# A four-layer graph network on one core: exponentials without a bias column, attention's gathered products one chunk later, feature copies apart from their transposes

## The chip, the cores and the metric

The kernel runs on one core of one Trainium2 chip. The core has a matrix engine (TensorE, PE in the profile, with its weight loads as PEld), a vector engine (DVE), an engine for functions and copies (ScalarE, ACT), a general engine (GpSimd, POOL), and a queue engine (SyncE, SP) that here starts transfers. Each engine works through its own instructions strictly in order, and waits on the others by semaphores. Transfers started on SP's and POOL's queues run on 16 DMA engines.

The metric is the device time of one execution in microseconds. The time before the change is the median of three executions, 1510.31 us (1508.68 to 1513.79).

## The reference, cut to what matters

Input are features `x` (4096 nodes, 64 features) and a symmetric, sparse weight matrix `adj` of 4096 x 4096. Four layers follow, each wrapped as `x = layernorm(x + layer(x, adj))`:

```python
# layer 0: Chebyshev polynomial of adj
terms = [x, L @ x]
for _ in range(2, 4): terms.append(2 * (L @ terms[-1]) - terms[-2])
return einsum('kni,kio->no', stack(terms), weight)

# layer 1: two gated cells, one fed by sums over neighbours, one by attention
edge_output = gru_cell(node_support, h, w_ih_e, w_hh_e, b_ih_e, b_hh_e)
edge_support = softmax(scores by the sign of adj) * adj @ (h @ W)
node_output = gru_cell(edge_support, h, w_ih_n, w_hh_n, b_ih_n, b_hh_n)

# layer 2: each neighbour weighted by 0.5 ** (rank from the last one)
w = mask * where(pos > 0, 0.5 ** (k - pos), 0)
return w @ (x @ weight) + bias

# layer 3: hyperbolic aggregation
log_ij = logmap(x_i, x_j)            # arctanh of a norm, for every pair i, j
agg = einsum('ij,ijc->ic', adj / deg, log_ij)
return expmap(0, agg @ weight + bias)
```

In the last layer every one of the 4096 x 4096 pairs needs a factor with a square root and an inverse hyperbolic tangent. The kernel forms them from a pair's number v: w = v squared less one, its root by a logarithm and an exponential of half of it, the logarithm of v plus the root, and the inverse root by another exponential.

## The kernel before, in words

The matrix is handled in 8 groups of 512 rows by 8 chunks of 512 columns, tiles of 128 x 4 x 512 numbers (1 MB). The program is written in an order, but a scheduler places the instructions on each engine by its own estimate of when they are ready; instructions wrapped in `in_order` keep their written order among each other. An engine then never leaves the placed order. So an edit can move instructions that it doesn't touch.

*Layer 0* (to about 570 us). PE transposes every tile (L633), ACT copies it out (L640), POOL's queue stores it (L664), and three passes of products follow; in the third, the groups of rows are taken from both ends (7, 0, 6, 1, 5, 2, 4, 3). When a group's pass is over, `third_weighed` weighs its sum (ACT copies the bank out to `t_h` at L545, PE multiplies at L552, DVE adds at L708). One chunk later `after_third` calls `normed_third`: PE turns the sum back (L492), DVE and ACT make the layer norm (root on ACT, L265), DVE centres the features in `nat_a` (L315) and splits them in three parts (L236 to L244, with a scratch tile `sp_rest`, tag `t0`). Four chunks after that `turned_third` calls `turn_pairs` (L226): POOL sets a column to one (L229), ACT copies the group's features to `with_ones` (L230), PE transposes them in pairs (L233), ACT copies them out (L234). `with_ones` shares tag `t0` and its two buffers with `sp_rest`. The last group (3) does this within attention, as its fourth step.

*Attention, layer 1* (to about 850 us). Per group of rows, over 8 chunks: DVE makes the masks `pos` (L477), POOL's queue stores them (L773), PE accumulates `p_ps` (L1041, L1049) and `a_ps` (L1058). After a group, `group_end` gives six parts of work, one for each following chunk (`steps_of`, L1001; popped at L1097). Part one: gates of the edge cell for two halves h of the group (PE L835, L842; tanh on ACT L851; the rest on DVE L856 to L858), scores and their exponentials (L906, L907), `gathered` of half 0 (PE, L932), shares (DVE, to L925), new state. Part two: `shared` of half 0 (ACT copies with a scale, L941), `gathered` and `shared` of half 1, gates of the node cell (PE L835) and their sum (DVE L865). The results of gates and of `gathered` go in turn to the two buffers of the tag `post`, each of two banks, so that half 0 of `gathered` follows half 0 of the edge gates in one buffer, and half 0 of the node gates follows half 0 of `gathered`.

*Layer 2* (to about 1050 us). Here `seam` holds small steps of other work, one taken per block of columns (L1345): first the last group's `group_end`, each step by itself. While `seam` isn't empty (`busy`, L1344), both evictions of `cnt_ps` per half block are on ACT (L1320), else one of them is on DVE (L1322).

*Layer 3* (to the end). 36 tiles on and above the diagonal, two units of 128 x 1024 each (8 of the 72 units are half as large). Per unit: PE forms v (L1435), ACT squares it (L1444), PE adds a very large number to pairs on opposite sides of the unit sphere (L1454), DVE subtracts one with a floor (L1462), ACT takes the logarithm (L1633) and the exponential of its half (L1634), DVE adds v (L1658), ACT takes the inverse root by an exponential (L1660) and the logarithm (L1669), DVE clips and multiplies (L1643), multiplies into `adj` (L1646) and into its transposed copy (L1482, after transposes L1480), and PE sums (L1496, L1508). So that numbers stay in the logarithm's domain, its input is scaled by 2^-20 and each exponential gives that back by a bias read from a column in memory, `half_shift`.

Of the kernel before, what the change touches and what calls it, by code (L numbers as in the profile page):

```python
# [9 lines left out]
F32 = mybir.dt.float32  # L10
# [3 lines left out]
AF = mybir.ActivationFunctionType  # L14
ALU = mybir.AluOpType
# [6 lines left out]
MIN_NORM = 1e-15  # L22
# [5 lines left out]
V_FLOOR = 2.0**-21  # L28

OPPOSITE = 2.0**60  # L30

# [6 lines left out]
TANH_ONE = 20.0  # L38
LN_SHIFT = 20

# [20 lines left out]
def gnn4_kernel(  # L61
# [21 lines left out]
    nc = tc.nc  # L83
    P = 128
    N, F = x.shape
    NB = N // P
    GB = 4
# [44 lines left out]
    nc.vector.memset(neg_inf, NEG_INF)  # L132
    half_shift = const.tile([P, 2], F32, name="half_shift")
    nc.vector.memset(half_shift[:, 0:1], 0.5 * LN_SHIFT * math.log(2.0))
    nc.vector.memset(half_shift[:, 1:2], -0.5 * LN_SHIFT * math.log(2.0))
    one_col = const.tile([P, 1], F32, name="one_col")
    nc.vector.memset(one_col, 1.0)

    pair = const.tile([P, F], F32, name="pair")
# [69 lines left out]
    def gblocks(g):  # L209
        return slice(g * GB, (g + 1) * GB)  # L210
# [8 lines left out]
    def to_rows(pool, src, w):  # L219
# [4 lines left out]
        return ps  # L224

    def turn_pairs(pool, g):  # L226

        t = sm.tile([P, GB, F], F32, name="with_ones", tag="t0")
        nc.gpsimd.memset(t[:, :, F - 1], 1.0)  # L229
        nc.scalar.copy(t[:, :, 0 : F - 1], nat_a[:, gblocks(g), 0 : F - 1])  # L230
        ps = pool.tile([P, GB // 2, P], F32, name="post", tag="post")
        for m in range(GB // 2):
            nc.tensor.transpose(ps[:, m, :], t[:, 2 * m : 2 * m + 2, :].rearrange("p b f -> p (b f)"), ident)  # L233
        nc.scalar.copy(tr_x[:, g * GB // 2 : (g + 1) * GB // 2, :], ps)  # L234
# [249 lines left out]
    def mine(g):  # L484

        return slice(g % 2 * F, g % 2 * F + F)
# [18 lines left out]
    with tc.tile_pool(name="acc", bufs=1) as acc_p, tc.tile_pool(  # L505
# [204 lines left out]
        def after_third(g):  # L710
            normed_third(g, acc_t[mine(g), g // 2, :], ps_p)

        def turned_third(g):
# [93 lines left out]
    def group_end(g, Q, nb, tl, sums, a_t, wq, by_ln=False):  # L807
# [179 lines left out]
        def of(h, *parts):  # L987
            return lambda ps_p: [part(ps_p, h) for part in parts]

        return [  # L990
            [of(0, edge_gates)], [of(0, edge_tanh)], [of(0, edge_rest), of(1, edge_gates)], [of(1, edge_tanh)],
            [of(1, edge_rest), scores], [tanh_n, score_exps, of(0, gathered)], [shares],
            [lambda ps_p: new_state(edge)],
        ], [
            [of(0, shared), of(1, gathered)], [of(1, shared)], [of(0, node_gates)], [of(0, node_sum)],
        ], [
# [8 lines left out]
    def attention(signed, cols_p, sg, tl, ps_a, ps_p):  # L1005
# [67 lines left out]
        ahead = [masks(*order[n]) for n in range(lead)]  # L1073
        steps = [nothing, nothing, nothing, lambda ps_p: turn_pairs(ps_p, last_row)]
        for n, (g, c) in enumerate(order):
# [83 lines left out]
    def constants3():  # L1159
# [12 lines left out]

        nc.vector.tensor_scalar(w[:, 0 : F - 1], pair[:, 0 : F - 1], 1.0, -4.0, ALU.add, ALU.mult)
        nc.vector.tensor_scalar(w[:, 0 : F - 1], w[:, 0 : F - 1], not_last, None, ALU.mult)
        nc.vector.tensor_copy(w[:, F - 1 : F], pair[:, F - 1 : F])
        nc.vector.memset(to_right, 0.0)
# [191 lines left out]
    with tc.tile_pool(name="o3", bufs=1) as op, tc.tile_pool(name="cols3", bufs=3) as cols_p, tc.tile_pool(  # L1368
# [90 lines left out]
        def less_one(n):  # L1459
            if n < NU:  # L1460
                w = ws[n][:, :, columns(n)]
                nc.vector.tensor_scalar(w, w, -1.0, V_FLOOR * (V_FLOOR + 2.0), ALU.add, ALU.max)  # L1462

# [58 lines left out]
        def factors(ps_p):  # L1522

            t = sm.tile([P, NB], F32, name="plus")
            nc.vector.tensor_scalar_max(t, deg, 1e-8)
            nc.vector.reciprocal(t, t)
            plus = sm.tile([P, NB], F32, name="plus")
            nc.vector.tensor_scalar_max(plus, inside, MIN_NORM)
            nc.vector.tensor_tensor(t, t, plus, ALU.mult)
            nc.vector.tensor_copy(kappa[:, 1, :], t)  # L1530
            nc.vector.tensor_tensor(t, t, rabs, ALU.mult)
            nc.vector.tensor_tensor(kappa[:, 0, :], t, inside, ALU.mult)
# [88 lines left out]
        while n < NU + 2 or turns or gathers:  # L1621
# [5 lines left out]
            if n < NU:  # L1627
                if n % 2 == 0:
                    fs[n // 2] = fp.tile([P, CB, GW], F32, name="f3")
                w, cs = ws[n][:, :, columns(n)], columns(n)  # L1630
                rts[n] = el.tile([P, HB, GW], F32, name="rt3")
                rt = rts[n][:, :, cs]
                nc.scalar.activation(w, w, AF.Ln, scale=2.0**-LN_SHIFT)  # L1633
                nc.scalar.activation(rt, w, AF.Exp, bias=half_shift[:, 0:1], scale=0.5)  # L1634
                square(n + 1)
                opposite(n + 1)
# [20 lines left out]
            if n < NU:  # L1657
                nc.vector.scalar_tensor_tensor(rt, vs[n][:, :, cs], 1.0 + V_FLOOR, rt, ALU.max, ALU.add)  # L1658
                product(n + 2)
                nc.scalar.activation(w, w, AF.Exp, bias=half_shift[:, 1:2], scale=-0.5)  # L1660
            late = turn(late_turns.pop(n)) if n in late_turns else []
# [5 lines left out]
            if 0 < n <= NU:  # L1667
                rt = rts[n - 1][:, :, columns(n - 1)]
                nc.scalar.activation(rt, rt, AF.Ln)  # L1669
            if seam:  # L1670
# [56 lines left out]
```

## Time and profile before

| | |
|---|---|
| median of three executions | 1510.31 us |
| the profiled execution | 1508.28 us |
| its span, first to last instruction | 1506.2 us |
| PE busy | 1366.3 us, 91% |
| DVE busy | 1030.4 us, 68% |
| ACT busy | 764.6 us, 51% |
| POOL busy | 123.2 us, 8% |
| chain that ended last | PE 55%, ACT 16%, DVE 16%, DMA 7% |

The profile comes from one execution. Its page gives each engine's busy time, its busy tenths in 40 slices of the span, the chain of work that ended last (followed back from the last instruction to what released it), and the costliest groups of instructions. A group's row reads: line, engine, operation, output from input, shapes, count, busy time, mean of one in ns, and the idle time just before it with what ended it. Other views give the busy time of each engine within a window, who waited for whom, and the timeline. The shares of the whole span are means over stages with different limits: ACT's 51% is under 30% in attention and over 90% in the last layer.

### The profile page before, as it was taken

To read this page: it belongs to the slowest core of one execution; us is meant where nothing else is said; L and a number is where in the kernel's file an instruction comes from. 1 tells how busy PE (TensorE), PEld (TensorE's weight loads), DVE (VectorE), ACT (ScalarE), POOL (GpSimd) and SP (SyncE) were. 2 spreads that over 40 slices of the span, in tenths; PEclk is the share of its full clock that TensorE was granted. 3 is DMA by queue.
4 is the path that set the end of the run, shared out by engine and by line. 5 is a ranking of instruction groups with operands and counts; after the bars stand their busy time and mean duration, and the time that the engine had idled before them with its cause. 6 is when DMAs were issued, how large, how long until landed. Compare 5 with 4: busy or idle time off the path is not lost.

```text
span 1506.2 us, 19544 instructions
## 1 busy us (share of the span) xinstructions
PE 1366.3 (91%) x7124; PEld 609.0 (40%) x7124; DVE 1030.4 (68%) x2008; ACT 764.6 (51%) x1301; POOL 123.2 (8%) x206
## 2 busy tenths in 40 slices
PE   5899999999999989888999999999788889888894
PEld 3555555564444323333333332333233334344342
DVE  5999999885000556666776422444999999999995
ACT  3554444442000111122222277564789999999993
POOL 4101000000000002222222100000000000000000
PEclk8999999999999999999999999999899999999997
DMA  9999999996678898888988655551434453544420
GB/s 292 415 406 413 411 411 400 387 353 273 238 280 272 344 403 308 290 299 296 338 328 312 207 171 174 169 168 58 196 140 171 160 204 140 202 165 171 154 105 11
DMA packets 103361, 385.40 MB, mean 256 GB/s; under 512 B 16340, under 2 KB 17368, under 8 KB 71256
## 3 DMA queue, kind: packets, MB, share of 16 engines
q1 hardware_dynamic: 84256, 296.78, 55.0%
q0 software_dynamic: 15616, 85.73, 13.9%
q10 hardware_dynamic: 3384, 1.56, 0.4%
q8 instruction: 58, 0.95, 0.3%
q14 instruction: 47, 0.39, 0.1%
HBM read 297.26 MB, written 85.20 MB: 254 GB/s over the span
## 4 chain that ended last, share of the span: by engine, by line
PE 55%; ACT 16%; DVE 16%; DMA 7%; issue 3%; SPq 1%; ACTq 0%; POOL 0%; DVEq 0%; POOLq 0%
PE tp L633 7%; PE pass L541 7%; PE w_ps L541 6%; PE a_ps L1058 4%; PE pass L534 4%; PE cnt_ps L1315 4%; DMA raw<-in_adj_dram 4%; PE acc_ps L1271 3%; PE h_ps L534 3%; PE p_ps L1041 2%; ACT w L1633 2%; PE post L552 2%; ACT rt L1634 2%; ACT rt L1669 2%; DVE at_m L1482 2%
## 5 line engine op out<-in xcount | busy, mean ns | idle before, releaser
L640 ACT COPY at<-tp 128x512 f32<-128x512 f32 x256 | 132.5, 600 | 132.3 <-issue 93.2
L1320 ACT ACTIVATE wt<-cnt_ps 128x512 uint16<-128x512 f32 x206 | 114.6, 596 | 72.2 <-PE cnt_ps L1315 67.9
L1496 PE MATMUL sums_ps<-at_d,nat_c 128*64 128x512 f32 x288 | 145.6, 628 | 3.0 <-DVE at_d L1475 2.0
L633 PE MATMUL tp<-ident,raw 128*128 128x128 f32 x1024 | 131.9, 282 | 15.2 <-DMA raw<-in_adj_dram 10.1
L666 DVE TENSOR_REDUCE dpart<-raw 128x4 f32<-128x2048 f32 x64 | 145.5, 2273 | 0.1
L668 DVE TENSOR_REDUCE lows<-raw 128x1 f32<-128x2048 f32 x64 | 145.4, 2272 | 0.0
L633 PEld LDWEIGHTS tp<-ident,raw 128*128 128x128 f32 x1024 | 115.0, 143 | 54.8 <-issue 30.2
L1058 PE MATMUL a_ps<-at,nat_a 128*64 128x512 f32 x512 | 126.3, 621 | 2.9 <-DVE at L1024 2.9
L477 DVE TENSOR_SCALAR pos<-at 128x2048 fp8e4<-128x2048 f32 x72 | 87.7, 1234 | 50.0 <-DMA at<-adj_t 43.8
L1508 PE MATMUL sums_ps<-at_m,nat_c 128*64 128x512 f32 x224 | 111.5, 621 | 0.0
L1435 PE MATMUL v_ps<-rv,tr_a 64*128 64x512 f32 (+1 forms) x288 | 82.8, 654 | 28.0 <-DVE rt L1658 27.5
L541 PE MATMUL w_ps<-at,cheb_n 128*128 128x512 f32 x224 | 101.1, 595 | 0.0
L541 PE MATMUL pass<-at,cheb_n 128*128 128x512 f32 x224 | 100.0, 604 | 0.7 <-DVE cheb_n L694 0.7
L1658 DVE SCALAR_TENSOR_TENSOR rt<-v_ps,rt 128x1024 f32<-128x1024 f32 x72 | 83.6, 1163 | 9.0 <-ACT rt L1634 8.8
L1315 PE MATMUL cnt_ps<-m,follow 128*64 128x512 fp8e4 x480 | 81.5, 391 | 4.8 <-ACT wt L1320 1.7
L1643 DVE SCALAR_TENSOR_TENSOR f<-rt,w 128x1024 f32<-128x1024 f32 x72 | 83.1, 1163 | 3.9 <-ACT rt L1669 3.9
L1646 DVE TENSOR_TENSOR at_d<-at_d,f 128x1024 f32<-128x1024 f32 x72 | 83.6, 1161 | 0.2
L1322 DVE TENSOR_SCALAR wt<-cnt_ps 128x512 uint16<-128x512 f32 x50 | 34.6, 692 | 67.9 <-PE cnt_ps L1315 67.9
L1634 ACT ACTIVATE rt<-w,half_shift 128x1024 f32<-128x1024 f32 x72 | 78.9, 1100 | 0.5
L1660 ACT ACTIVATE w<-w,half_shift 128x1024 f32<-128x1024 f32 x72 | 78.8, 1098 | 0.5
L1482 DVE TENSOR_TENSOR at_m<-post,at_m 128x512 f32<-128x512 f32 x112 | 74.4, 685 | 4.5 <-PE post L1480 4.5
L1480 PE MATMUL post<-ident,f 128*128 128x128 f32 x448 | 68.1, 284 | 9.5 <-DVE at_m L1482 8.5
(396 smaller groups left out, 2228.8 us busy)
## 6 DMA issues: line engine op xcount, KB each, us to landing
at<-adj_t SPq DMA_DIRECT2D x122, 1024.0 KB, 5.9
raw<-in_adj_dram SPq DMA_DIRECT2D x64, 1024.0 KB, 13.1
adj_t<-at POOLq DMA_DIRECT2D x64, 1024.0 KB, 8.1
at_d<-adj_t SPq DMA_DIRECT2D x36, 1024.0 KB, 4.8
at_m<-adj_t SPq DMA_DIRECT2D x28, 1024.0 KB, 7.0
mask_t<-pos POOLq DMA_DIRECT2D x64, 256.0 KB, 5.7
m<-mask_t SPq DMA_DIRECT2D x120, 128.0 KB, 2.8
m<-mask_t SPq DMA_DIRECT2D x60, 256.0 KB, 4.1
```

What stands on the lines that cost most here:

```text
L534: in_order(nc.tensor.matmul(ps[q * F : (q + 1) * F, :], lhsT=cheb_n[:, jb, k, :], rhs=rhs, start=first, stop=last, skip_group_check=True,))
L541: in_order(nc.tensor.matmul(ps, lhsT=cheb_n[:, jb, k : k + 2, :], rhs=rhs, start=first, stop=last))
L633: in_order(nc.tensor.transpose(tp[:, cols(b)], raw[:, b, cols(k)], ident))
L640: nc.scalar.copy(at[:, k, :], tp)
L666: in_order(nc.vector.tensor_reduce(dpart[:, g, c, :], raw, AX.X, ALU.add))
L668: in_order(nc.vector.tensor_reduce(lows[:, n : n + 1], raw.rearrange("p b j -> p (b j)"), AX.X, ALU.min))
L1058: in_order(nc.tensor.matmul(ps[q * F : (q + 1) * F, :], lhsT=nat_a[:, c * CB + k, 0:F], rhs=parts[q if signed else 0][:, k, :], start=(c = ...
L1315: in_order(nc.tensor.matmul(cnt[a][r * HP : (r + 1) * HP, :], lhsT=follow, rhs=chunks[c][odd][2 * a + r][:, k, :], start=(h == 2 * NB - 1) ...
L1320: in_order(nc.scalar.activation(wt[odd][a], cnt[a], AF.Relu, scale=-128.0))
L1496: in_order(nc.tensor.matmul(bank[0:F, :], lhsT=nat_c[:, j * CB + k, :], rhs=own[t][:, k, :], start=(i == j and k == 0), stop=(j == seq[-1] ...
L1508: in_order(nc.tensor.matmul(bank[F:P, :], lhsT=nat_c[:, above * GB + k, :], rhs=mirrored[tm][:, k, :], start=(k == 0 and above == seq[0]), ...
L1634: nc.scalar.activation(rt, w, AF.Exp, bias=half_shift[:, 0:1], scale=0.5)
```

## The change

In the last layer v itself is scaled by 2^-10 (in the small weights that PE uses for it, `constants3`), so that its square carries 2^-20 and no shift is needed: logarithm and exponentials lose scale and bias, the column `half_shift` goes, and the constants that v and w meet carry the scale, as does the last logarithm (an immediate scale). The number for opposite pairs is 2^50, not 2^60.

In `group_end`, `gathered` of half 0 moves from part one to the front of part two, a chunk later; in layer 2's seam it is a step of its own, and the shift by one step moves two evictions of `cnt_ps` from DVE to ACT.

`turn_pairs` is cut in two: `put_ones` (the fill and the copy to `with_ones`) is called right after `normed_third`, and the transposes stay where they were written. `with_ones` gets a tag and two buffers of its own.

```diff
-OPPOSITE = 2.0**60
+OPPOSITE = 2.0**50
-LN_SHIFT = 20
+SCALE = 2.0**-10
...
-    half_shift = const.tile([P, 2], F32, name="half_shift")
-    nc.vector.memset(half_shift[:, 0:1], 0.5 * LN_SHIFT * math.log(2.0))
-    nc.vector.memset(half_shift[:, 1:2], -0.5 * LN_SHIFT * math.log(2.0))
...
-    def turn_pairs(pool, g):
-        t = sm.tile([P, GB, F], F32, name="with_ones", tag="t0")
+    ones_in = {}
+    def put_ones(g):
+        ones_in[g] = t = sm.tile([P, GB, F], F32, name="with_ones")
         nc.gpsimd.memset(t[:, :, F - 1], 1.0)
         nc.scalar.copy(t[:, :, 0 : F - 1], nat_a[:, gblocks(g), 0 : F - 1])
+    def turn_pairs(pool, g):
+        t = ones_in[g]
...
         def after_third(g):
             normed_third(g, acc_t[mine(g), g // 2, :], ps_p)
+            put_ones(g)
...
-            [of(1, edge_rest), scores], [tanh_n, score_exps, of(0, gathered)], [shares],
-            [lambda ps_p: new_state(edge)],
+            [of(1, edge_rest), scores], [tanh_n, score_exps], [shares], [lambda ps_p: new_state(edge)],
         ], [
-            [of(0, shared), of(1, gathered)], [of(1, shared)], [of(0, node_gates)], [of(0, node_sum)],
+            [of(0, gathered)], [of(0, shared), of(1, gathered)], [of(1, shared)], [of(0, node_gates)], [of(0, node_sum)],
...
-        steps = [nothing, nothing, nothing, lambda ps_p: turn_pairs(ps_p, last_row)]
+        steps = [nothing, nothing, lambda ps_p: put_ones(last_row), lambda ps_p: turn_pairs(ps_p, last_row)]
...
-        nc.vector.tensor_scalar(w[:, 0 : F - 1], pair[:, 0 : F - 1], 1.0, -4.0, ALU.add, ALU.mult)
+        nc.vector.tensor_scalar(w[:, 0 : F - 1], pair[:, 0 : F - 1], 1.0, -4.0 * SCALE, ALU.add, ALU.mult)
...
-                nc.vector.tensor_scalar(w, w, -1.0, V_FLOOR * (V_FLOOR + 2.0), ALU.add, ALU.max)
+                nc.vector.tensor_scalar(w, w, -SCALE * SCALE, V_FLOOR * (V_FLOOR + 2.0) * SCALE**2, ALU.add, ALU.max)
...
-            nc.vector.tensor_scalar_max(plus, inside, MIN_NORM)
+            nc.vector.tensor_scalar(plus, inside, MIN_NORM, SCALE, ALU.max, ALU.mult)
...
-                nc.scalar.activation(w, w, AF.Ln, scale=2.0**-LN_SHIFT)
-                nc.scalar.activation(rt, w, AF.Exp, bias=half_shift[:, 0:1], scale=0.5)
+                nc.scalar.activation(w, w, AF.Ln)
+                nc.scalar.activation(rt, w, AF.Exp, scale=0.5)
...
-                nc.vector.scalar_tensor_tensor(rt, vs[n][:, :, cs], 1.0 + V_FLOOR, rt, ALU.max, ALU.add)
+                nc.vector.scalar_tensor_tensor(rt, vs[n][:, :, cs], (1.0 + V_FLOOR) * SCALE, rt, ALU.max, ALU.add)
...
-                nc.scalar.activation(w, w, AF.Exp, bias=half_shift[:, 1:2], scale=-0.5)
+                nc.scalar.activation(w, w, AF.Exp, scale=-0.5)
...
-                nc.scalar.activation(rt, rt, AF.Ln)
+                nc.scalar.activation(rt, rt, AF.Ln, scale=1.0 / SCALE)
```

More of the change, by code (lines that the diff above doesn't have):

```diff
@@ L1171, in constants3 @@
         nc.vector.tensor_scalar(not_last, pair[:, F - 1 : F], -1.0, 1.0, ALU.mult, ALU.add)
-        nc.vector.tensor_scalar(w[:, 0 : F - 1], pair[:, 0 : F - 1], 1.0, -4.0, ALU.add, ALU.mult)
+        nc.vector.tensor_scalar(w[:, 0 : F - 1], pair[:, 0 : F - 1], 1.0, -4.0 * SCALE, ALU.add, ALU.mult)
         nc.vector.tensor_scalar(w[:, 0 : F - 1], w[:, 0 : F - 1], not_last, None, ALU.mult)
-        nc.vector.tensor_copy(w[:, F - 1 : F], pair[:, F - 1 : F])
+        nc.vector.tensor_scalar_mul(w[:, F - 1 : F], pair[:, F - 1 : F], SCALE)
         nc.vector.memset(to_right, 0.0)
```

## The prediction

> **What bounds the kernel now.** I read the page first (span, engines, slices), then windows around each place that the change touches, then who waited for whom there, then single stretches of the timeline.
>
> ```profile
> span 1506.2 us, 19544 instructions
> ...
> PE   5899999999999989888999999999788889888894
> DVE  5999999885000556666776422444999999999995
> ACT  3554444442000111122222277564789999999993
> ```
>
> TensorE (PE) is at eight tenths or more in 37 of 40 slices; from slice 29 on (about 1060 us, the last layer) DVE and ScalarE (ACT) are at nine tenths too, and PE has its waits. The busy times of that stretch, 1060 to 1470 us (columns: length, then busy us of PE, PEld, DVE, ACT, POOL, then clock and DMA), and who DVE waited for there:
>
> ```profile
> 1060.00:1470.00 410.00, 356.51 (x1695) 151.58 (x1691) 385.51 (x651) 391.40 (x533) 0.62 (x2) 0.96 0.43 162
> ```
> ```profile
> DVE rt L1658 <- ACT rt L1634: 8.8, 10, 2.8
> DVE w L1462 <- ACT w L1444: 5.6, 8, 1.4
> DVE f L1643 <- ACT rt L1669: 3.9, 6, 1.1
> DVE at_m L1482 <- PE post L1480: 3.7, 6, 1.3
> ```
>
> ACT is idle 18.6 of 410 us, DVE 24.5: two engines almost equally full, and DVE's waits are mostly for ACT (18.3 of them). The chain that ended last in this stretch, by line (the answer breaks off there):
>
> ```profile
> by line: ACT w L1633 8.5%; ACT rt L1634 8.3%; ACT rt L1669 8.1%; DVE at_m L1482 7.5%; ACT w L1660 7.3%; DVE rt L1658 7.0%; PE sums_ps L1496 6.8%; ACT w L1444 6.7%; DVE at_d L1646 5.6%; DVE f L1643 5.1%; issue 5.0%; PE v_ps L1435 4.1%; DVE w
> ```
>
> The exponentials L1634 and L1660 hold 15.6% of it. In attention (580 to 845 us) PE is the bound but for stretches at 570 to 685 us that end on loads; its waits there, and one group's timeline (start, length, instruction):
>
> ```profile
> ACT gin L941 <- DVE share L925: 16.2, 7, 2.4
> ...
> PE post L932 <- DVE n L858: 11.5, 7, 3.0
> ```
> ```profile
> 754.14 0.89 PE L932 MATMUL post<-wq,a_t 128*128 128x192 f32 x4 [1.12 <-DVE n L858]
> ...
> 758.13 0.81 PE L932 MATMUL post<-wq,a_t 128*128 128x192 f32 x4
> 758.93 0.70 PE L835 MATMUL post<-whh_n,tr_a 64*128 64x256 f32 x4
> ```
> ```profile
> 755.25 0.30 ACT L907 ACTIVATE none<-top,neg_inf 128x4 f32<-128x4 f32 x1 [0.20 <-DVE top L900]
> 755.65 0.21 ACT L906 ACTIVATE share<-share 128x4 f32<-128x4 f32 x1
> 758.14 1.58 ACT L941 ACTIVATE gin<-post,share 128x192 f32<-128x192 f32 x4 [2.29 <-DVE share L925]
> ```
>
> The reader is to see that node gates (L835) stand ready to start just when ACT has emptied the first gathered bank. In the third pass (500 to 570 us) PE waits little, 4.2 us of it for the features' copy:
>
> ```profile
> 551.35 0.41 PE L233 MATMUL post<-ident,with_ones 128*128 128x128 f32 x2 [3.17 <-ACT with_ones L230]
> ```
> ```profile
> 550.80 0.40 ACT L230 COPY with_ones<-nat_a 128x252 f32<-128x252 f32 x1 [4.38 <-DVE sp_lo L244]
> ```
>
> **The change part by part.**
>
> *Exponentials without bias.* L1634 and L1660, 72 each, lose the per-partition bias. Price: in the timeline above two exponentials of 128x4 stand side by side, 0.30 us with a bias column, 0.21 without. At 128x1024, where ACT runs without a gap, one instruction starts 1.04 us after an exponential with bias and 0.948 us after a logarithm without, so 0.093 us each. 144 of them: 13.4 us of ACT's time. The other edits here (constants in L1462, L1658, L1669, the scale in `factors` and `constants3`) leave count, shapes and engines as they are; two small fills at the start go, off any path. What of 13.4 us reaches the end? First way: the chain has 15.6% of 410 us = 64 us in these lines, 61 instructions of 1.04, so 61 x 0.093 = 5.7. Second way: ACT's busy time falls to 378.0, below DVE's 385.5; if the fuller engine stays idle as long as now (18.6), the stretch takes 404.1, 5.9 less. What is late next is DVE, with PE's waits for L1658 behind it. I take 6. Ends: 13.4 (ACT alone bounds) and below nothing, because the order of instructions in this layer is remade on ACT, DVE and PE: the logarithm L1669 follows its own L1634 and L1660 at once in 5 places, not 1, where DVE's 1.22 us between them doesn't fit under 0.95; ACT's waits of this kind are 6.0 us in 7 now, 0.86 each, so 4 more are +3.4. Against that, L1633 stands one instruction behind its square L1444 in 7 places, not 14. I put the order at nothing.
>
> The Trainium skill, "Perfetto Trace Analysis", section "Identifying the Most-Contended Engine", has the engine of highest occupancy as the one whose relief pays; read strictly, ACT with 95.5% against DVE's 94.0% would return all 13.4 us, and the sum below would be -13.9. The waits shown above, with DVE only 5.9 us less busy, speak against so much.
>
> *Gathered products one chunk later.* `gathered` of half 0 (two products, four passes, no DMA) leaves the step behind edge gates and stands with half 1 in the next chunk. Orders of DVE, ACT, POOL and SP in the branch that runs stay as they are. PE's wait of 1.12 us goes (11.5 in 7 groups). But node gates of half 0 write the bank that gathered half 0 has just filled, and it is emptied by ACT's first two L941, which wait for the shares, and these for DVE's L925, ending at 758.03. Nothing of that moves: the second L941 ends at 758.88. PE would reach L835 at 758.93 - 1.12 = 757.8 and wait until about 758.95. The same holds at 645, 720, 788 and 821 us: nothing won in five groups. In the two others, where the wait is 2.87 and 3.04 (at 606 and 685), L835 stands at 612.58 and 691.33, while L941's second copy ends at 610.88 and 689.66: 1.6 won in each, 3.2; loads are awaited soon after (at 629 and 664 PE waits 2.0 and 2.9 for DVE behind them), so I count half, -1.5. Ends: -11.5 and +0.7 (0.1 of signalling in each of seven).
>
> *Copies apart from transposes.* `put_ones` (a fill of 0.11 on POOL, a copy of 0.40 on ACT) comes four chunks ahead, in buffers of its own, so it no longer waits for `sp_lo` (L244). On POOL two fills go ahead of layer 0's stores, which wait for ACT anyway (214 us); in attention the fill stays behind the third mask store, and its buffer's last reader is two rows back. Not free: the order of PE changes, the transposes L233 stand one chunk earlier, and ACT's queue has the copy ahead of the root L265 and of `t_h` (L545). Rows 6 and 1: the turn of row 1 (L492) now stands directly behind L552, and waits for DVE's L708, which ends at 522.3: 0.8. Row 6's transposes are reached at about 524.7, while its features are centred at 525.1 and copied by 525.7: 1.1; row 1's about 0.45. Old waits 0.76 and 0.27 go: +1.3. Rows 5 and 2: the copy of row 5 can start at 541.3 (L315 ends 541.2) and is ahead of the `t_h` copy that ran at 540.35: PE is 1.35 late. The 3.17 wait shrinks to about 1.1, as row 2 is centred 5 us after its L492, with one transposing step and one chunk of 3.65 between: -2.1, so -0.7. Sum +0.6, taken as +1, since DVE's interleaving of two rows changes as well. Ends: -4.2 (all waits go, none comes) and +4.8 (0.8 + 1.1 + 0.45 + 1.35 + 1.1, none goes).
>
> *Layer 2's seam* runs 26 small steps, not 25. Two evictions of 0.69 go from DVE to ACT (0.60 each). ACT is busy 85 of 140 us in 900 to 1040, PE 136: nothing, and up to 1.2 if PE waited for both.
>
> Sum: -6 - 1.5 + 1 = -6.5. The profiled execution took 1508.28 us (2.1 beside its span), so 1501.8; it lies 2.0 under the median of 1510.31, so 1503.8 for the median.
>
> **The rivals.**
> 1. *ACT bounds the last layer alone.* For: ACT's idle time of 18.6 us is the smallest. Against: DVE at 385.5. It gives -13.4 - 1.5 + 1 = -13.9: 1496.4. Chance 0.20.
> 2. *DVE takes over at once,* and ACT's gain turns into waits of ACT for L1658 and L1462. For: DVE's 94%. Against: DVE waits 18.3 us for ACT. With 1 us won there: -1.5, 1508.8. Chance 0.19.
> 3. *Attention's waits do go,* as the change's words suggest: -11.5 in place of -1.5, 1493.8. It needs shares ahead of 757; nothing in DVE's order brings that. Chance 0.06.
> 4. *Slower: the remade order of the last layer.* In-order queues block where ACT's instruction stands ahead of what DVE can feed it. It decides when a unit (there are 72) loses over 0.15 us, as 72 x 0.15 = 10.8 outweighs 6 and leaves +4.5 or so: 1514.8 and above, say 1516. Against it is the shorter list of tight places. Chance 0.08.
>
> **How the numbers follow.** About 0.3%, 4.5 us, is what a measurement of this kernel can tell from no change. The forecast has 0.47; its own range, from the 4 to 8 us that the last layer may return and 2 either way elsewhere, is 1499 to 1508, and a seventh of it lies within 0.3% (above 1505.8). Faster: 0.40 + 0.20 + 0.06 = 0.66. Same: 0.07 + 0.19 = 0.26. Slower: 0.08. The range reaches to 1493 (rival 1 with 3 us more from the third pass) and to 1510 (rival 2 and a little): it leaves out most of rival 4 and the far ends.
>
> **What would show it.** After: exponentials of 128x1024 at 1.05 us like the logarithms; ACT busy near 378 and DVE near 385 in a last layer of about 404 us; no wait of PE on L932, and in its place one of about 1.1 us on node gates for ACT's `gin`; a period of 33.7 us per group as now (754.14 to 787.84); the third pass as long as now or 1 us longer. Wrong if the last layer shortens by over 10 us or under 2, or if the groups' period falls by 1 us.

## The result and the profile after

| | before | after |
|---|---|---|
| median, timed together | 1509.06 us (6 executions) | 1497.12 us (6 executions, 1492.16 to 1503.91) |
| ratio, 95% interval | | 0.9931 (0.9907 to 0.9955) |
| once more, in a later set of runs: medians | 1507.59 us (35) | 1501.34 us (12, 1492.48 to 1507.66) |
| ratio, 95% interval | | 0.9944 (0.9920 to 0.9968) |
| profiled execution, its span | 1508.28, 1506.2 us | 1492.16, 1490.4 us |

The change makes the kernel faster by 8 to 10 us, where 6.5 were forecast. The two profiled executions differ by 16 us. That is more than the change gives: the profiled execution of after is the fastest of 18, and other executions of the same program ran up to 15 us longer. So stages are compared below over all profiled executions that share the part in question, not between two.

The page of the changed kernel: span, and the busy tenths of three engines in 40 slices.

```profile
span 1490.4 us, 19538 instructions
...
PE   5999999999999989889999899999788899889884
...
DVE  5989998886000467666677422435899999999995
ACT  3554444342000110222222277564789999999993
```

The picture is the old one: PE nearly full to slice 28, then DVE and ACT at nine tenths. The last layer (first product L1439 to last logarithm L1673) in this execution: length, then busy us of PE, PEld, DVE, ACT, POOL, clock, DMA share, GB/s.

```profile
1051.40:1454.40 403.00, 353.53 (x1706) 151.49 (x1705) 385.93 (x657) 380.39 (x530) 0.62 (x2) 0.98 0.44 168
```

The costliest groups of ACT there, and then who DVE waited for there (us in total, times, longest):

```profile
L1664 ACT ACTIVATE w<-w 128x1024 f32<-128x1024 f32 x72 | 72.3, 1006 | 0.7
L1638 ACT ACTIVATE rt<-w 128x1024 f32<-128x1024 f32 x72 | 72.3, 1005 | 0.6
```
```profile
DVE w L1466 <- ACT w L1448: 5.4, 6, 1.8
DVE rt L1662 <- ACT rt L1638: 3.4, 5, 2.5
DVE at_m L1486 <- PE post L1484: 3.2, 3, 1.4
DVE f L1647 <- ACT rt L1673: 2.1, 4, 0.6
```

An exponential takes as long as a logarithm now; the two groups lost 13.1 us (78.9 + 78.8 before). DVE, whose work is unchanged (387.3 before, over 412.1 us), is now the fuller engine, and its waits for ACT's first exponential fell from 8.8 to 3.4.

In attention, the timeline of one group shows the wait in its new place. PE's products (L937, now both halves together) no longer wait; its node gates (L840) do, for ACT's `gin`:

```profile
749.91 1.46 PE L937 MATMUL post<-wq,a_t 128*128 128x192 f32 x8
752.71 0.70 PE L840 MATMUL post<-whh_n,tr_a 64*128 64x256 f32 x4 [1.34 <-ACT gin L946]
```
```profile
751.92 1.36 ACT L946 ACTIVATE gin<-post,share 128x192 f32<-128x192 f32 x4 [2.29 <-DVE share L930]
```

The stages, in us. "Attention, loads" runs from the first group's copy of `p_t` to the fourth's, "steady" from there to the eighth's. Means; the number of profiled executions and their range in brackets. An execution is counted for a stage where that stage has the part in question and no other edit.

| stage | without the part | with it | difference | forecast |
|---|---|---|---|---|
| second and third pass, first `t_v` copy to the first `p_ps` | 193.9 (3: 193.7 to 194.2) | 192.8 (11: 192.6 to 194.2) | -1.1 | +1 |
| attention, loads | 114.7 (3: 113.4 to 116.0) | 111.7 (8: 109.4 to 114.1) | -3.0 | -1.5 |
| attention, steady | 134.9 (3) | 134.9 (8: 134.7 to 135.6) | 0 | 0 |
| layer 2 | 208.5 (3: 205.9 to 210.6) | 209.4 (8: 205.9 to 210.6) | +0.9, in the spread | 0 |
| last layer | 412.2 (4: 411.5 to 412.8) | 405.4 (6: 403.0 to 406.8) | -6.8 | -6 |
| from there to the end | 37.5 (4: 36.7 to 38.5) | 35.9 (6: 35.6 to 36.0) | -1.7 | 0 |

These differences sum to -11.7; the times say -10.4 (-14.0 to -6.8) and -8.4 (-12.1 to -4.8).

Part of this is the granted clock. In these traces it is 1.00 or 0.50 and nothing between, and it falls for 3.4 us at a time or for several times that; 3.4 us at half clock are 1.7 us of PE's work lost. In "attention, loads", where PE has waits of up to 3.9 us, the time at half clock orders all fourteen profiled executions:

| at half clock | length of "attention, loads" |
|---|---|
| 3.4 us | 109.4 |
| 6.8 us | 110.7 to 112.7 (6 executions) |
| 10.2 us | 113.3, 113.4 |
| 11.8 us | 114.1 |
| 13.7 us | 114.6, 116.0 (the latter the kernel before) |
| 20.5 us | 120.6, 120.8 (two experiments below, "both halves in one buffer") |

Layer 2 is 205.9 us long where the clock never falls, 208.9 to 209.3 with 6.8 us at half clock and 210.3 to 210.6 with 10.2.

### The profile page after: what moved, and what is told of

Read it like the earlier page. It is cut to its first block, busy times and chain, and to the rows that moved or that the text cites. A ratio compares the mean times of both kernels' runs of the same rounds, so it can differ in the third digit from the quotient of the medians.

```text
span 1490.4 us, 19538 instructions
## 1 busy us (share of the span) xinstructions
PE 1355.1 (91%) x7124; PEld 609.0 (41%) x7124; DVE 1026.1 (69%) x2004; ACT 753.2 (51%) x1303; POOL 122.7 (8%) x206
## 4 chain that ended last, share of the span: by engine, by line
PE 51%; DVE 20%; ACT 16%; issue 6%; DMA 5%; ACTq 1%; POOL 0%; SPq 0%; DVEq 0%; POOLq 0%
PE tp L637 7%; PE pass L545 7%; PE w_ps L545 7%; PE cnt_ps L1319 4%; PE acc_ps L1275 4%; PE pass L538 3%; PE h_ps L538 3%; PE post L556 2%; DVE at_m L1486 2%; ACT w L1637 2%; DMA at<-adj_t 2%; DVE f L1647 2%; ACT w L1448 2%; ACT rt L1638 2%; ACT wt L1324 2%
## 5 line engine op out<-in xcount | busy, mean ns | idle before, releaser
L1500 PE MATMUL sums_ps<-at_d,nat_c 128*64 128x512 f32 x288 | 140.6, 607 | 2.4 <-DVE at_d L1479 1.8
L1062 PE MATMUL a_ps<-at,nat_a 128*64 128x512 f32 x512 | 122.4, 605 | 2.9 <-DVE at L1028 2.9
L1512 PE MATMUL sums_ps<-at_m,nat_c 128*64 128x512 f32 x224 | 107.3, 600 | 0.0
L1439 PE MATMUL v_ps<-rv,tr_a 64*128 64x512 f32 (+1 forms) x288 | 79.4, 629 | 22.6 <-DVE rt L1662 22.4
L1673 ACT ACTIVATE rt<-rt 128x1024 f32<-128x1024 f32 x72 | 72.4, 1005 | 9.5 <-DVE rt L1662 9.2
L1637 ACT ACTIVATE w<-w 128x1024 f32<-128x1024 f32 x72 | 72.0, 1002 | 5.0 <-DVE w L1466 5.0
```

Of the source, the lines that this page charges most:

```text
L1062: in_order(nc.tensor.matmul(ps[q * F : (q + 1) * F, :], lhsT=nat_a[:, c * CB + k, 0:F], rhs=parts[q if signed else 0][:, k, :], start=(c = ...
L1500: in_order(nc.tensor.matmul(bank[0:F, :], lhsT=nat_c[:, j * CB + k, :], rhs=own[t][:, k, :], start=(i == j and k == 0), stop=(j == seq[-1] ...
L1512: in_order(nc.tensor.matmul(bank[F:P, :], lhsT=nat_c[:, above * GB + k, :], rhs=mirrored[tm][:, k, :], start=(k == 0 and above == seq[0]), ...
```

## The experiments

Each ratio is to the kernel before, run on the same chip in the same set, with its 95% interval. Line numbers of an experiment can be one to three off those of the changed kernel; the operations tell which is which.

### Each part alone

**The exponentials and scales alone**: the kernel before with all hunks of the diff that concern `SCALE`, `OPPOSITE` and `half_shift`.

> The kernel before with the edits of the exponentials and scales alone; attention and the third pass as before. From the two traces: 9 us under the kernel before, all of it in the last layer. By the prediction's term: 6 under. If only the whole change gains that much there: less than 4 under.

Measured: median 1499.89 us, ratio 0.9938 (0.9921 to 0.9955), that is -9.4 us (-11.9 to -6.8). Last layer 403.5, end of it to end of program 36.0. This part alone gives as much as the whole change.

**The gathered products alone**:

```diff
-            [of(1, edge_rest), scores], [tanh_n, score_exps, of(0, gathered)], [shares],
-            [lambda ps_p: new_state(edge)],
+            [of(1, edge_rest), scores], [tanh_n, score_exps], [shares], [lambda ps_p: new_state(edge)],
...
-            [of(0, shared), of(1, gathered)], [of(1, shared)], [of(0, node_gates)], [of(0, node_sum)],
+            [of(0, gathered)], [of(0, shared), of(1, gathered)], [of(1, shared)], [of(0, node_gates)], [of(0, node_sum)],
```

> The kernel before with the gathered products one chunk later alone; last layer in the old order with the old price. By the prediction: 1.5 us under the kernel before, half a us to 1.6 in each of the two groups whose loads bind (stretches of 606 and 685 us). From the two traces: about 5 under, 2 and 3 in those two groups, nothing in the other groups, where PE's wait of 1.1 moves from the gathered products to the node gates and becomes 1.3. Nothing in the other stages.

Measured: 1507.38 us, ratio 1.0005 (0.9980 to 1.0030). Loads stretch 112.7, 1.9 under the mean of those without it; steady groups 135.6. In the time the part is nothing that can be told, and 5 us are excluded. What the two profiles seemed to show here (-5.2 over attention) was mostly the spread of the groups that wait for loads: with the same order of instructions they took anything from 109.4 to 114.1 us.

In the two load-bound groups where the forecast had 1.6 us each to win, PE's waits of 2.87 and 3.04 came back in full at the node gates, 2.87 and 3.25. What the part won in the first of them is mostly the clock's. In the kernel before, the products behind the wait took 3.46 us; without the wait in front of them the same eight took 1.94 (the kernel before, then this one):

```profile
606.14 0.89 PE L932 MATMUL post<-wq,a_t 128*128 128x192 f32 x4 [2.87 <-DVE n L858]
606.96 3.46 PE L1058 MATMUL a_ps<-at,nat_a 128*64 128x512 f32 x8
```
```profile
602.94 1.94 PE L1057 MATMUL a_ps<-at,nat_a 128*64 128x512 f32 x8
```

**The copies apart from their transposes alone** (`put_ones` and its calls):

> The kernel before with the features' copies apart from their transposes alone. By the prediction: 1 us longer in the third pass (order of the rows' copies). From the two traces: 1 shorter. Both within what a few rounds can tell from nothing in the whole time (0.3% is 4.5 us); the third pass's last t_h copy in the profile, 566.3 before, tells it: 567.3 by the one, 565.2 by the other.

Measured: 1508.06 us, ratio 0.9992 (0.9973 to 1.0011). The stage of the second and third pass took 192.7; `t_h` of the last row comes 188.9 after the first `t_v` copy, against 190.1 before: 1.2 shorter, in the direction opposite to the forecast. PE's waits from 495 to 571 us in the kernel before, and in this one:

```profile
PE post L233 <- ACT with_ones L230: 4.2, 3, 3.2
PE post L552 <- ACT t_h L545: 2.8, 4, 0.7
PE p_ps L1041 <- DVE pos L477: 0.7, 1, 0.7
PE post L492 <- ACT tr_a L234: 0.5, 1, 0.5
```
```profile
PE post L558 <- ACT t_h L551: 4.2, 4, 2.0
PE post L239 <- ACT with_ones L232: 2.5, 3, 1.2
PE post L498 <- DVE acc_t L714: 0.8, 1, 0.8
PE p_ps L1048 <- DVE pos L483: 0.7, 1, 0.7
PE post L498 <- ACT tr_a L240: 0.5, 1, 0.5
```

Waits for `with_ones` lost 1.7, the two that the forecast added came as forecast (`t_h` +1.4, `acc_t` +0.8): +0.5 in sum, and yet the stage is shorter. The windows of the same stretch, the `t_h` copy of row 0 to the first `p_ps`, of the kernel before and of this one, show where it comes from:

```profile
499.20:570.10 70.90, 62.65 (x277) 20.77 (x274) 45.24 (x185) 12.05 (x29) 1.94 (x8) 0.97 0.93 372
```
```profile
500.70:570.40 69.70, 60.99 (x277) 20.34 (x274) 44.97 (x185) 12.08 (x29) 1.66 (x6) 1.00 0.95 378
```

The same number of products (277) keeps PE busy 1.7 us less, at a granted clock of 1.00, not 0.97. Right behind the old wait of 3.17 us (it ends at 551.35) the clock is low, for 3.4 us from 552.6 on (here without the two ends):

```profile
552.70:556.00 3.30, 3.30 (x11) 0.86 (x9) 0.00 (x0) 0.00 (x0) 0.00 (x0) 0.50 0.96 377
```

Half of 3.4 is the 1.7 us. One other execution tells this from the waits: the one with old order and old price in the next section has the new waits of this stage one by one, but its clock fell here as well, and the stretch took 71.2 us, with PE busy for 62.53.

### The last layer: price or order

Without its bias operand an exponential also costs less in the scheduler's estimate, so the change has two effects: cheaper instructions, and a new order of instructions on ACT, DVE and PE. Four kernels separate them. They differ in the last layer alone; old price means a bias column of zeros in memory.

```diff
+    zero_col = const.tile([P, 1], F32, name="zero_col")
+    nc.vector.memset(zero_col, 0.0)
...
-                nc.scalar.activation(rt, w, AF.Exp, scale=0.5)
+                nc.scalar.activation(rt, w, AF.Exp, bias=zero_col[:, 0:1], scale=0.5)
...
-                nc.scalar.activation(w, w, AF.Exp, scale=-0.5)
+                nc.scalar.activation(w, w, AF.Exp, bias=zero_col[:, 0:1], scale=-0.5)
```

With this in the source the old order comes back: ACT, DVE and PE run the last layer's instructions in the sequence of the kernel before. For the two mixed cases the operand is exchanged after the order is fixed, in the finished program:

```python
for block in nc.m.functions[0].blocks:
    now = list(block.instructions)
    for k, inst in enumerate(now):
        if ...:   # the 144 exponentials
            now[k] = dataclasses.replace(inst, ins=(inst.ins[0], bias, *inst.ins[2:]))
    block.instructions = now
```

> The changed kernel once more, as the mark for the three beside it and to see how far its time moves from chip to chip: about 12 us under the kernel before (ratio 0.992), last layer about 9 us shorter than before's.

> The changed kernel with a column of zeros as the bias of both kinds of exponential. The planner prices the column, so it puts the last layer's instructions back in exactly the order of the kernel before: old price, old order, new scales. If price or order or both make the gain of the last layer, its stretch (first v_ps product to the last logarithm) is as long as before's, 412 us within 1, the exponentials take 1.10 us, and the whole is 9 us longer than the changed kernel, that is 4 to 6 us under the kernel before. If it stays shorter than before's by more than 3, the gain came from elsewhere (the new scales of the VectorE operations, or the clock).

> The same as the run with the column in the old order, but the zero column is taken off the 144 exponentials after the planner has set the order: new price, old order. Price theory (the prediction's): as fast as the changed kernel within 1 us, last layer about 403 us, exponentials 1.00 us. Order theory (the prediction's rival 4 turned round: the remade order itself gains): last layer within 2 us of the old 412, whole 7 to 9 us slower than the changed kernel. Halves: the prediction's -6 for the price alone would leave it 3 us behind the changed kernel.

> The changed kernel in its own order, with the zero column put on the 144 exponentials after the planner has set the order: old price, new order. Price theory: 8 to 9 us slower than the changed kernel, last layer 411 to 413 us. Order theory: as fast as the changed kernel within 2 us. By the prediction's -6 for the price, 6 us slower and 3 of the gain left to the order.

| | ratio (interval) | last layer | 48 units in its middle |
|---|---|---|---|
| old order, old price | 0.9988 (0.9971 to 1.0006) | 412.5 | 272.6 |
| old order, new price | 0.9967 (0.9949 to 0.9985) | 408.4 | 270.2 |
| new order, old price | 0.9996 (0.9976 to 1.0016) | 417.7 | 274.5 |
| new order, new price (the change) | 0.9944 (0.9920 to 0.9968) | 406.4 | 267.7 |

The last column runs from the 17th square to the 65th. It leaves out the start of the layer, where executions differ, and repeats well: 272.3 to 272.8 in four kernels with old order and price, 267.5 to 267.7 in six with new order and price. The two mixed cases were profiled once each. With old order and price the layer is as long as in the kernel before (412.1) although v is scaled, so the new constants alone give nothing. These windows in the kernel before, with the new price alone, with the new order alone, and in the change:

```profile
1149.10:1421.90 272.80, 242.17 (x1172) 103.19 (x1172) 256.72 (x400) 264.85 (x364) 0.00 (x0) 0.98 0.47 174
```
```profile
1146.60:1416.80 270.20, 241.51 (x1170) 102.94 (x1170) 255.64 (x399) 256.56 (x364) 0.00 (x0) 0.98 0.47 175
```
```profile
1143.20:1417.70 274.50, 245.87 (x1170) 102.78 (x1170) 255.57 (x399) 265.87 (x363) 0.00 (x0) 0.98 0.46 173
```
```profile
1139.90:1407.50 267.60, 241.12 (x1170) 101.86 (x1170) 254.65 (x400) 257.32 (x365) 0.00 (x0) 1.00 0.47 176
```

ACT's busy time (the number behind DVE's 256.72 in the first row) falls by 8.3 and 8.6 with the price. In the old order the stretch gets 2.4 shorter by it (272.6, the mean of the four, to 270.2), in the new order 6.9. The new order without the new price costs 1.9; with it, it gains 2.6. So neither theory holds alone: price and order work together, and the new order is good only with the price that it was made for. With the new order alone DVE waits more for PE and for the square:

```profile
DVE at_m L1488 <- PE post L1486: 5.6, 6, 1.9
DVE w L1468 <- ACT w L1450: 5.5, 4, 1.8
DVE rt L1664 <- ACT rt L1640: 5.2, 7, 2.2
```

against 2.6, 4.2 and 6.8 in the old order. The clock does not make this split: 10.2 us of the stretch ran at half clock in the first three rows alike; with new order and price it was none or 3.4 us, and that moved the stretch by at most 0.2. Of the 2.6 (and of the 6.9) a few tenths may be the clock's, an estimate from these 0.2. In whole times the same signs show (price -3.2 in the old order and -7.8 in the new, of ratios times 1507.6), but there the four intervals overlap too much to tell the order's share; the split rests on the middle units. Of the 5.6 us by which the last layer with new order and old price (417.7) exceeds that of the kernel before, 0.9 lie in front of the middle units, 1.8 in them and 3.0 behind, where the clock was 0.93, against 1.00.

### What bounds the last layer now

Two kernels in the changed kernel's own order, each with work taken off one engine.

> The changed kernel in its own order with ScalarE's work in the last layer cut by a further 13.4 us: the last logarithm of 64 units runs on 768 of its 1024 columns (a quarter of the logarithms is left out), 0.21 each by the rows 1005 ns for 1024 columns and 584 for 512. Last layer of the changed kernel 403 to 406.5, VectorE's busy time there 386. ScalarE alone bounds: 13 shorter. VectorE alone bounds: 0 to 1 shorter. Two engines nearly level, waiting for one another: 2 to 6 shorter.

> The changed kernel in its own order with VectorE's work in the last layer cut by 12.8 us: the products of the slopes into the adjacency run on 832 of 1024 columns in 64 units (19% of these products left out), 0.2 each by the rows 1211 ns for 1024 columns and 670 for 512. ScalarE alone bounds: 0 to 1 shorter. VectorE alone bounds: 12 to 13 shorter. Two engines nearly level: 4 to 9 shorter, and more than the cut of ScalarE gives, since VectorE has 386 of busy time there and ScalarE 380.

Measured: 1494.81 us, ratio 0.9911 (0.9885 to 0.9937) with ACT's work cut, 1493.63 us, 0.9917 (0.9901 to 0.9934) with DVE's. Last layer 402.1 and 402.5, against 405.4 (403.0 to 406.8). Each was profiled once. A shortened logarithm took 816 ns on the mean of all 72, a shortened product 977. The middle units, ACT's cut and then DVE's:

```profile
1140.40:1405.30 264.90, 240.37 (x1170) 101.34 (x1170) 254.00 (x400) 248.68 (x364) 0.00 (x0) 1.00 0.48 179
```
```profile
1141.10:1407.50 266.40, 242.09 (x1172) 102.19 (x1172) 247.13 (x400) 257.13 (x363) 0.00 (x0) 0.99 0.48 178
```

Cutting ACT by 8.6 gives 2.7, cutting DVE by 7.5 gives 1.2. Either engine alone as the bound is out: each cut turns into waits of the engine that was cut. ACT's waits for DVE rose from 5.9 (after) to

```profile
ACT rt L1673 <- DVE rt L1662: 10.6, 20, 1.0
```

and with DVE's work cut, DVE's waits for PE's transposes rose from 3.2 to

```profile
DVE at_m L1486 <- PE post L1484: 6.5, 10, 1.7
```

Two engines in a fixed order, level in load, wait for one another, and a part is held by PE. The bracket of 4 to 9 expected for DVE was too high: about half of DVE's new idle time in the middle units (3.3 of 6.3 us) is the wait of `at_m` for transposes. DVE is the fuller engine after the change, and yet a cut there returned no more than one of ACT did: 2.9 against 3.3 us over the whole layer, 1.2 against 2.7 in the middle units.

### The wait that moved, in attention

**Both halves of the gathered products in one buffer**, so that node gates find the other one free. First with the halves interleaved, then each in a bank of its own (the diff is the second's):

```diff
+        def place(ps, h, i):
+            return ps[:, h, i * H3 : (i + 1) * H3] if Q == 1 else ps[:, i, 0 : Q * H3]
...
-                got[bs.start] = ps = new(ps_p)
+                if Q == 1 and h:
+                    got[bs.start] = ps = got["both"]
+                else:
+                    got[bs.start] = got["both"] = ps = new(ps_p)
```

> The changed kernel, same order of instructions, with both halves of a chunk's gathered products in one buffer (the second half at column 192), so that the node gates of a chunk find a buffer that ScalarE's gin copies don't hold. If PE's wait at the node gates (1.3 to 1.75 us in each of the seven groups behind the first) is for that buffer and PE bounds the group: period of the steady groups 33.7 to about 32.5, 5 to 11 us under the changed kernel in all. If the next thing behind (VectorE's shares and states, about as busy there) is late right away, the wait moves to another product and the period stays 33.7: within 1 us of the changed kernel. If the later buffers hold the second half's gin back on VectorE: up to 0.5 longer a group, 4 slower.

> The changed kernel, same order of instructions, with both halves of a chunk's gathered products in one PSUM buffer, each half in a bank of its own (in the run with one buffer the two halves interleaved, so the second half's products had to wait for the first half's gin copies: 1.99 us a group at the gathered products, period 34.5). Theory: PE's wait at the node gates (1.34 in a steady group) was for a buffer held by gin, so it goes, and PE's period falls from 33.7 to 32.4 to 33.2, 3 to 9 us in all under the changed kernel. Rival: the second node gates or the next chunk's gates then wait for the one buffer that all four gin copies hold, and the period stays 33.7.

Measured: 1509.84 us, ratio 1.0017 (0.9997 to 1.0037), and 1514.03 us, 1.0046 (1.0031 to 1.0062): both slower than the change, and the second slower than the kernel before. Attention took 289.2 and 287.4 us against 274.3 on the mean of eight, a steady group 34.5. PE in one group, halves interleaved and then in own banks:

```profile
760.86 0.81 PE L941 MATMUL post<-wq,a_t 128*128 128x192 f32 x4
763.66 0.92 PE L941 MATMUL post<-wq,a_t 128*128 128x192 f32 x4 [1.99 <-ACT gin L950]
764.50 0.70 PE L840 MATMUL post<-whh_n,tr_a 64*128 64x256 f32 x4
```
```profile
766.25 0.92 PE L943 MATMUL post<-wq,a_t 128*128 128x192 f32 x4 [1.99 <-ACT gin L952]
```

Node gates wait no more, as meant. But the second half's products wait for the first half's `gin` copies, banks apart or not. The likely reason is that this program's semaphores guard the buffer as a whole; the trace gives the wait, not its reason. And the wait got longer, 1.99 for 1.34: it stands after one half's products (0.81), not after both (1.46), so PE arrives 0.65 earlier at an event that stays where it was, 1.34 + 0.65 = 1.99. Neither theory had that. Whether the halves could run without this wait wasn't tried. About 9 of the 15 and 13 us that attention lost lie in the groups that wait for loads, and most of these are the clock's: 20.5 us there at half clock, against 7.4 on the mean of the eight.

**The shares first.** What sets the event is DVE: between the sum z (L927) and its reciprocal (L928) stands the comparison `pos` of a later chunk. Writing the new state ahead of the shares moves it behind:

```diff
-            [of(1, edge_rest), scores], [tanh_n, score_exps], [shares], [lambda ps_p: new_state(edge)],
+            [of(1, edge_rest), scores], [tanh_n, score_exps], [lambda ps_p: new_state(edge)], [shares],
```

> The changed kernel with one more move: a group's new edge state is issued before its shares, which puts the 1.22 us comparison of a later chunk's adjacency (pos) behind the reciprocal and the share on VectorE instead of between them; nothing else moves on any engine. In the changed kernel's steady group the sum z ends at 750.4, pos runs from 750.30 to 751.52, the share ends at 751.8, gin starts at 751.92 and PE's node gates wait 1.34. Theory (that pos, not gin's length or the buffers, sets this wait): the share ends about 1.0 earlier, PE's wait falls from 1.34 to about 0.3, the period of the steady groups from 33.7 to about 32.7, and the whole is 5 to 7 us under the changed kernel, 14 to 16 under the kernel before. Rival (PE waits elsewhere at once): pos itself ends 0.5 later and PE waits for it, or the loads can't follow the shorter period (their queue moves 320 GB/s in these groups); the period stays within 0.3 of 33.7, and the whole is as the changed kernel's.

Measured: 1491.59 us (1490.32 to 1496.03), ratio 0.9897 (0.9879 to 0.9914). DVE and PE in one group of the changed kernel, then of this one:

```profile
783.98 1.22 DVE L481 TENSOR_SCALAR pos<-at 128x2048 fp8e4<-128x2048 f32 x1
785.11 0.17 DVE L928 RECIPROCAL z<-z 128x4 f32<-128x4 f32 x1
785.31 0.16 DVE L930 TENSOR_TENSOR share<-share,z 128x4 f32<-128x4 f32 x1
...
786.38 0.70 PE L840 MATMUL post<-whh_n,tr_a 64*128 64x256 f32 x4 [1.33 <-ACT gin L946]
```
```profile
781.89 0.18 DVE L928 RECIPROCAL z<-z 128x4 f32<-128x4 f32 x1
782.10 0.16 DVE L930 TENSOR_TENSOR share<-share,z 128x4 f32<-128x4 f32 x1
782.18 1.23 DVE L481 TENSOR_SCALAR pos<-at 128x2048 fp8e4<-128x2048 f32 x1
...
783.16 0.70 PE L840 MATMUL post<-whh_n,tr_a 64*128 64x256 f32 x4 [0.33 <-ACT gin L946]
```

The wait falls by 1.0 as expected, and three of the four steady groups take 32.6 to 32.7 us, the other 33.3, where a wait of 0.96 is left; all four together 131.3, not 134.7 to 135.0. The theory holds: this one comparison set PE's wait, and PE bounds these groups. Against the change's two ratios it is 5 to 7 us faster (0.9897 / 0.9931 and / 0.9944, of 1508), though the two were not run in one set; the steady groups account for 3.5 of it. It is the fastest version of this study, 15.5 us (13.0 to 18.2) under the kernel before.

## Why the prediction was right or wrong

It forecast 1503.8, and faster. The kernel is faster, at 1497 to 1501, inside the range of 1493 to 1510.

*Exponentials, the price of one: right.* 0.093 us each were forecast; the rows went from 1100 to 1005 ns. ACT's busy time in the last layer fell from 391.9 to 380.4 (378 forecast), by 11.5, where the two rows lost 13.1; DVE's stayed at 386 (385).

*Last layer, -6: the sum right, the terms not.* It measured -6.8 and a length of 405.4 on the mean (404.1 forecast). But the step "I put the order at nothing" failed. In the 48 middle units the old order returns 2.4 of 8.3 us of ACT's time, 29%, and the new order adds 2.6. The chain's count of 61 instructions, 5.7, was too much for the old order, where the whole layer got 3.8 shorter: work off that chain was nearly as late. With the new price in the old order DVE's waits for PE's transposes rose from 2.6 to 5.9 in the middle units, and ACT's for L1658 from 2.8 to 4.9. The new order made it up, so that the sum of -6 came out close by luck. The second way took DVE as the bound, with as much idle time as ACT had before (18.6); DVE's idle time is 17.1 (403.0 - 385.9) in the profile of after and 20.0 in its second one, so that figure came close without a reason why the waits should carry over. The further 1.7 behind the last logarithm was in no term. It goes with the order rather than the price: 36.7 to 38.7 us in five executions with the old order (38.7 with the new price), 35.6 to 36.5 in the nine with the new one (36.5 with the old price). Part of the spread within each order is the clock again.

*Rival 1, ACT alone, -13.9:* out, as the exponentials' 13.1 us gave 6.8, and of a further cut there the layer returns a quarter to a third. The Trainium skill, "Perfetto Trace Analysis", section "Identifying the Most-Contended Engine", names the engine of highest occupancy as the one to relieve first. Relief of that engine did pay here, but about half of what it was relieved by, as the second engine was 5 us behind in 412. *Rival 2, DVE at once:* out by the same -6.8. *Rival 4, the order loses:* its mechanism exists, at 1.9 us in 48 units (0.04 a unit, not the 0.15 needed), but only with the old price.

*Attention, -1.5: the mechanism right in the steady groups, not in the two others.* The wait of 1.12 at the gathered products did turn into one at the node gates, of 1.34, the steady groups stayed at 33.7, and rival 3 is out. The groups that wait for loads measured -3.0 on means whose ranges overlap, and -1.9 with this part alone; -1.5 can't be told from that. The term itself failed: 1.6 us were to be won in each of two groups because the node gates would wait 1.2 and 1.4, and with this part alone they waited 2.87 and 3.25, as long as the old waits. What the stage gained is mostly the clock's, which the forecast had at nothing: 12.5 us at half clock on the mean of the three without the part, 7.4 of the eight with it, worth about 2.5 of the 3.0. That the part always does this is not shown (10.2 to 13.7 without it, 3.4 to 11.8 with it), and why a wait brings the clock down in one execution and not in another stays open.

*Third pass, +1: wrong in sign, by 2.* The step's waits were right one by one, within 0.25: 0.86 and 0.45 for rows 6 and 1 (1.1 and 0.45 forecast), 1.20 for row 2 (1.1), 0.8 for `acc_t` (0.8), `t_h` +1.4 (1.35); their sum, +0.5, is the forecast's +0.6. What was missing is the term that the old wait of 3.17 us cost beyond itself: for 3.4 us behind it PE ran at half clock, 1.7 us of its busy time. Taking +0.6 up to +1 for DVE's interleaving was in the wrong direction.

*Layer 2's seam, 0:* nothing shown, 209.4 against 208.5 in a spread of 5 that goes with the clock.

## What to carry to other kernels

Where two engines are level, a cheaper instruction on one returns a part of its price, and how much depends on an order of instructions that fits the new durations: price and order must be tested apart and together. A wait that a move removes comes back at the next use of the same event; look for what sets the event, here one comparison wedged between two tiny operations, and move that. Compare stages over several executions, and the granted clock within them, before reading a gain off two profiles: here the two differed by 16 us where the change gives 8 to 10.

## What the runs showed of the hardware

- A wait of PE can cost more than its length. In all three profiled executions with the wait of 3.17 us in the third pass, the clock fell to 0.50 for 3.4 us, between 0.4 us before the wait's end and 1.3 behind it, and over that stretch of 71 us it was 0.97 to 0.98; in ten of the eleven without that wait it was 1.00. The eleventh had 0.98: its clock fell 1.4 us behind a wait of 1.97 that ends at 544.14, so a shorter wait can do it too, though the same wait didn't in the ten. The Trainium skill, "TensorE: Matmul & The Clock Gate", Part 1, has the clock fall after an idle window of about 3.4 us; the waits seen here are shorter than that.
- A column of zeros as bias costs what a column of numbers costs: 1097 ns against 1004 without, in the same order.
- The middle of the last layer repeats to 0.2 us in six profiled executions, while whole times of one program range over 15 us. What differs from execution to execution lies elsewhere: the groups of attention that wait for loads (109.4 to 114.1), layer 2 (205.9 to 210.6), the time up to the second pass's first `t_v` copy (375.1 to 379.0) and the first 16 units of the last layer (88.5 to 90.9). In the first two the length follows the time at half clock, 1.5 to 1.7 us for each fall of 3.4 us in layer 2.
